# Moving a pair's residual behind the zeroing in VectorE's queue, with the softmax sums in a layout for fewer DMAs

## The chip, the cores and the metric

The kernel runs on one core of one Trainium2 chip. The metric is the device time of one execution in microseconds (us); lower is better. Before the change it is 2849.32 us, the median of three runs (2841.83 to 2855.34).

## The reference

Two layers of attention over images of 16 x 256 x 32 x 32 in float32. In each layer the input is normalised in 16 groups over the last axis, projected to queries, keys and values of 4 heads (64 channels each), and attended with a relative position term; the result is added to the input.

```python
q, k, v = proj(Wq, bq), proj(Wk, bk), proj(Wv, bv)      # b, heads, 64, 1024
sim = jnp.einsum('bhdi,bhdj->bhij', q, k)
rel = (rel_h + rel_w).reshape(heads, d, n)
qpos = jnp.einsum('hdi,bhdj->bhij', rel, q)
attn = jax.nn.softmax(sim + qpos, axis=-1)
out = jnp.einsum('bhdn,bhmn->bhdm', v, attn)
...
x = x + _L0_conv_ref(_gn(x), ...)
x = x + _L1_conv_ref(_gn(x), ...)
```

## The kernel before, in words

The work is cut into 32 units, one per image and layer. A unit has two pairs of heads (`pr`), and a pair has two halves of 512 query positions, so a unit is four blocks; in `block(n)` the variable `b` is 0 to 3 and `half` is `b` modulo 2. The text calls them the first to the fourth block. The order of instructions on each engine is written out by hand: each engine works through its own queue strictly in the order in which `block` emits, and semaphores connect the queues. Moving a call in `block` therefore moves that instruction in its engine's queue and nothing else.

A block makes eight tiles of scores (`j` = 0 to 7), each of 128 keys by 2 heads by 512 queries. VectorE first writes the position term into PSUM (`seed`, L343), TensorE adds the products of keys and queries (`scores`, L379), and ScalarE takes exp into SBUF with a fixed shift in place of a maximum (L388). VectorE adds the eight tiles up in an accumulator (`add_up`, L397 and L399). TensorE multiplies the eight tiles with the values into `po`, in two stretches (`attend`, L413). The four two-bank PSUM tiles are called by the names in `ring`; a seed has to wait until ScalarE has read what stood in its tile before.

Between these stand pieces of later work: the projections, values and positions of the next pair or unit (`prepare`, L262, L292, L320), and the normalisation of the unit after the next, which is done by ScalarE (L187, L242). Its mean and its variance each take a small product on TensorE (`pm`, L207). That product adds into PSUM, so VectorE zeroes `pm` first (`zeroed`, L199). This happens in the third block for the mean and in the fourth for the variance. ScalarE then takes `neg` (L217) or `var` (L229) out of `pm`; the tile is one that the next block's second seed uses. GpSimd computes `rstd` and `nshift` from the variance (L231, L233). `token` (L163) is a tiny memset on GpSimd that keeps the two stretches of a product apart.

The softmax sums of a pair come out as follows. GpSimd's accumulating DMA folds the accumulator from 128 to 64 partitions (`fold`, L432); SyncE's DMA puts one quarter of it in the pair's `stack` (`stack_up`, L441); GpSimd's accumulating DMA adds the other quarter (`fold_again`, L448). One block after the pair's end, TensorE sums the stack over its partitions into the unused halves of `po` (`sums_of_pair`, L460). ScalarE copies `po` to `od` (`take_out`, L474 and L478): slots 0 and 1 of `od` hold the output of the two halves, slot 2 the sums. SyncE's DMAs spread the sums over 128 partitions in `den_all` (L485), VectorE takes reciprocals of 16 numbers per partition (`reciprocals`, L519), and SyncE's DMAs write them to `rd` in device memory (L522) and read them back, repeated over 64 partitions each, into `rden` (L525). All DMAs that SyncE issues leave in their order in its queue, and one whose source isn't ready holds up those behind it. Finally VectorE multiplies the output with `rden` and adds it with the bias to the image (`finish`, L536 and L537), the residual of the text. This is done once per pair, in the block with `half` = 1 of the following pair, so in each second and fourth block, for the pair `before`.

The last unit's second pair has no later work to interleave and is done by `block_without_pieces`.

Of the kernel before, what the change touches and what calls it, by code (L numbers as in the profile page):

```python
# [9 lines left out]
F32 = mybir.dt.float32  # L10
# [7 lines left out]
P = 128  # L18
HALF = 512
# [33 lines left out]
def fast_path(ctx, tc, sh, x, layers, out, W, den_all, token, good, flag):  # L53
# [26 lines left out]
    nc = tc.nc  # L80
    B, C, H, N, CC, NT, NH, D, GT = (
        sh.B, sh.C, sh.H, sh.N, sh.CC, sh.NT, sh.NH, sh.D, sh.GT
    )
# [317 lines left out]
    QUART = HALF // 2  # L401
# [32 lines left out]
    def stack_up(blk):  # L434

        u, pr, x = blk
        if x == 0:
            stacks[u, pr] = spool.tile([P, HALF], F32, tag="stack", name=f"stack_{u}_{pr}")
        for h in range(2):
            r0 = x * D + h * R  # L440
            nc.sync.dma_start(stacks[u, pr][r0 : r0 + R, :], accs[blk][:R, h, :])  # L441

    def fold_again(blk):
        u, pr, x = blk
        acc = accs.pop(blk)
        for h in range(2):
            r0 = x * D + h * R
            nc.gpsimd.dma_start(  # L448
                stacks[u, pr][r0 : r0 + R, :], acc[R:D, h, :], accum_op=ALU.add
            )  # L450

    def sums_of_pair(u, pr, po):

        stack = stacks.pop((u, pr))
        for x, rs in enumerate(QUARTERS):
            for c, cs in enumerate(QUARTERS):
                nc.tensor.matmul(  # L460
                    po[cs, 1 - x, QUART:],
                    W.two_ones[rs, :],
                    stack[rs, c * QUART : (c + 1) * QUART],
                    start=True, stop=True, skip_group_check=True,
                )

    def take_out(blk, po, sums_too=False):

        u, pr, half = blk
        if half == 0:  # L470
            outs[u, pr] = opool.tile([P, 3, HALF], F32, tag="od", name=f"od_{u}_{pr}")
        od = outs[u, pr]
        if not sums_too:
            nc.scalar.copy(  # L474
                od[:, half, :].rearrange("p (a n) -> p a n", a=2), po[:, :, :QUART]
            )
            return
        nc.scalar.copy(  # L478
            od[:, 0:3:2, :].rearrange("p z (a n) -> p z a n", a=2),
            po.rearrange("p a (z n) -> p z a n", z=2),  # L480
        )
        n = index[blk] - 2
        for x in range(2):
            for h in range(2):
                nc.sync.dma_start(  # L485
                    den_all[h * D : (h + 1) * D, n + x, :],
                    od[h * R : P : D, 2, (1 - x) * QUART : (2 - x) * QUART],
                )

    def sums_of_p(two, po):  # L490

# [22 lines left out]

    def reciprocals(u, pr, count=2):

        n = index[u, pr, 0]
        r8 = fpool.tile([P, 2, 8], F32, tag="r8", name=f"r8_{u}_{pr}")
        nc.vector.reciprocal(r8[:, :count, :], den_all[:, n : n + count, :])  # L519
        rd = dpool.tile([2, 2, HALF], F32, tag="rd", name=f"rd_{u}_{pr}")  # L520
        for x in range(count):
            nc.sync.dma_start(rd[:, x, :].rearrange("h (a b) -> h a b", b=8), r8[:, x, :])  # L522
        rdens[u, pr] = opool.tile([P, 2, HALF], F32, tag="rden", name=f"rden_{u}_{pr}")
        for h in range(2):
            nc.sync.dma_start(  # L525
                rdens[u, pr][h * D : (h + 1) * D, :count, :],
                rd[h : h + 1, :count, :].to_broadcast([D, count, HALF]),
            )

    def finish(u, pr):  # L530

        b, l = units[u]
        xs = xt[b][:, pr, :]
        o = outs.pop((u, pr))[:, 0:2, :].rearrange("p a n -> p (a n)")
        rden = rdens.pop((u, pr)).rearrange("p a n -> p (a n)")
        nc.vector.tensor_tensor(o, o, rden, ALU.mult)  # L536
        nc.vector.scalar_tensor_tensor(xs, o, W.bv[l][:, pr : pr + 1], xs, ALU.add, ALU.add)  # L537
        if l == NL - 1:
            nc.sync.dma_start(flat(out[b, pr * P : (pr + 1) * P]), xs)
# [75 lines left out]
    def block(n):  # L615
        blk = blocks[n]
        u, b = divmod(n, BPU)
        half = blk[2]
        before = blocks[n - 3][:2] if half == 1 and n > 2 else None
        after = blocks[n + 1] if n + 1 < len(blocks) else None  # L620
        previous = blocks[n - 1] if n > 0 else None
        one, two = u + 1 < NU, u + 2 < NU

        pieces = u + 1 < NU or b < 2
        if u + 1 == NU and b == 1:
            widen(u, 1)
        f0, f1, f2, f3 = ring
        folded = n - 1 < FOLDED
        if not pieces:
            return block_without_pieces(n, half)  # L630

        if previous:
            if half == 0:
                add_up(previous, 6)
            add_up(previous, 7)
        for j in range(1, 4):
            scores(blk, j)
        if b == 3 and u + 3 < NU and units[u + 3][0] not in xt:
            load_x(units[u + 3][0])
        (first, first_out), (second, second_out) = prepare(u, b)  # L640
        first(0)
        if b == 0 and one:
            norm_apply(u + 1, range(0, 1))
        if b == 2 and two:
            norm_sums(u + 2, range(8, 11))
        if b == 3 and two:
            norm_squares(u + 2, range(6, 9))
        seed(blk, 4, f1)
        scores(blk, 4)
        add_up(blk, 1)  # L650
        if before:
            reciprocals(*before)
        if half == 0:
            add_up(blk, 2)
        if b == 0 and one:
            norm_apply(u + 1, range(1, 5))
        if b == 1 and one:
            norm_apply(u + 1, range(15, G))
        if b == 2 and two:
            norm_sums(u + 2, range(11, G))  # L660
        if b == 3 and two:
            norm_squares(u + 2, range(9, 13))
        second(0)
        if half == 1:
            second_out()
        first.word()
        if previous and folded:
            fold(previous)
            stack_up(previous)
        first(1)  # L670
        first_out()
        seed(blk, 5, f0)
        scores(blk, 5)
        if half == 0:
            add_up(blk, 3)
            second.word()
            if previous and folded:
                fold_again(previous)
            second(1)
            second_out()  # L680
        seed(blk, 6, f1)
        scores(blk, 6)
        if half == 0:
            ring[2:] = f3, f2
        seed(blk, 7, ring[2])
        scores(blk, 7)
        if half == 1:
            add_up(blk, 2)
            add_up(blk, 3)
        add_up(blk, 4)  # L690

        if after:
            seed(after, 0, f0)
        if before:
            finish(*before)
        if n in check:
            next(checks)
        if b == 0 and one:
            norm_apply(u + 1, range(5, 10))
        if b == 3 and two:  # L700
            norm_squares(u + 2, range(13, G))
        po = psum2(ring[3], f"po_{n}")
        values_of_p = attend(blk, po)
        values_of_p(0)
        if two and b >= 2:
            mean, mean_out = (norm_mean if b == 2 else norm_var)(u + 2, zeroed(f1, f"pm_{n}"))
            mean(0)
        if after:
            scores(after, 0)
        values_of_p.word()  # L710
        if two and b >= 2:
            mean(1)
            values_of_p.word()
            mean_out()
        add_up(blk, 5)
        if after:
            for j in range(1, 4):
                seed(after, j, ring[j % 3])
        if half == 0:
            add_up(blk, 6)  # L720
        if b == 0 and one:
            norm_apply(u + 1, range(10, 15))
        if b == 1 and two:
            norm_sums(u + 2, range(0, 8))
        if b == 2 and two:
            norm_squares(u + 2, range(0, 6))
        values_of_p(1)
        if half == 1:
            if folded:
                fold_again(previous)  # L730
            take_out(blk, po)
            pos[n] = po
            return
        if n > 1:
            sums_of_pair(*blocks[n - 2][:2], po)
        take_out(blk, po, n > 1)
# [8 lines left out]
    def block_without_pieces(n, half):  # L745
# [43 lines left out]
        pd = psum2(f0, "pd")  # L789
        sums_on_rows(acc, pd)  # L790
        values_of_p(1)
        finish_half(u, pr, 0, outs[u, pr][:, 0, :], rdens[u, pr][:, 0, :])
        rden = rdens[u, pr][:, 1, :]
        nc.vector.reciprocal(rden, pd[:, 0, :])
        pd = psum2(f2, "pd_columns")[:, 0, : 2 * HALF // P]
        sums_on_columns(acc, pd)
# [417 lines left out]
```

## Time and profile before

| | |
|---|---|
| Time, median of 3 runs | 2849.32 us |
| Profiled execution, from first to last instruction | 2845.8 us |
| Mean granted TensorE clock | 0.981 |
| VectorE, 128 x 1024 float32 (L343, L399) | 1.23 and 1.22 us each |
| ScalarE, exp of 128 x 1024 (L388) | 1.12 us each |
| ScalarE, copy of 128 x 512 and 128 x 1024 (L474, L478) | 0.58 and 1.01 us each |
| VectorE, residual: L536, L537 | 1.22 and 1.29 us each, 63 of both |
| VectorE, memset of `pm` (L199) | 0.07 us each, 60 of them |
| SyncE, issue of one DMA (L485, L522, L525) | 0.57, 0.52 and 0.51 us, medians |

The profile is of one execution. In it, PE is TensorE's matmuls, PEld its weight loads, DVE VectorE, ACT ScalarE, POOL GpSimd and SPq the queue in which SyncE issues DMAs. A line of the list of waits names who waited for whom: engine, tile and line, then the total in us, the number of waits and the longest. A line of a timeline has the start, the time taken, the engine, the line and operation, the tiles (written on the left of the arrow, read on the right) and how many of the same stand together; in brackets stands how long the engine was idle before it and what released it. A line of busy time by stretch has the stretch, its length, each engine's busy time and number of instructions, the granted clock of TensorE (1.00 is full speed), the share of DMA and GB/s. A memset of zero takes so little time that a wait for it means a wait for what stands before it in its queue.

### The profile page before, as it was taken

Reading aid. Unit: us, or ns where it says so; the run is one execution under the profiler, and the core shown is the slowest. Engines: PE = TensorE matmul, PEld = TensorE weight load, DVE = VectorE, ACT = ScalarE, POOL = GpSimd, SP = SyncE. Lnnn points to the kernel's source line nnn. Section 1 sums busy time; section 2 is a strip of 40 time slices with the busy share of each in tenths; the row PEclk is TensorE's granted clock in tenths of the full one; section 3 lists DMA queues with packets and bytes.
Section 4 is the critical chain, followed back from the end, with each engine's and each line's share of the span. In section 5 each row is a group of like instructions: output and inputs, shape, how many; then the busy total and the mean of one; then the engine's idle time right before and its main releaser. Section 6 shows DMA issues by size and latency. Waiting matters only on the chain.

```text
span 2845.8 us, 86631 instructions
## 1 busy us (share of the span) xinstructions
PE 2642.4 (93%) x37970; PEld 1468.8 (52%) x37970; DVE 2427.1 (85%) x2200; ACT 1980.7 (70%) x3934; POOL 476.0 (17%) x825
## 2 busy tenths in 40 slices
PE   8999999899898999999999999999999989999998
PEld 4545555455454554545545555465554545545545
DVE  7888888888888888888888888888888888889898
ACT  6767677676676766767767667677676767767754
POOL 1111211111111111111111111111111111121110
PEclk9999999999999999999999999999999999999999
DMA  2122121221212212122131222222222222222221
GB/s 77 32 56 43 34 69 34 63 49 33 69 35 62 48 33 69 36 63 47 34 71 35 62 45 45 63 40 56 45 52 57 40 54 47 41 53 39 43 57 44
DMA packets 91615, 140.27 MB, mean 49 GB/s; under 512 B 49374, under 2 KB 50910, under 8 KB 91230
## 3 DMA queue, kind: packets, MB, share of 16 engines
q0 software_dynamic: 21824, 48.78, 11.7%
q1 hardware_dynamic: 69406, 85.88, 11.1%
q8 instruction: 299, 4.90, 0.7%
q14 instruction: 86, 0.70, 0.1%
HBM read 51.78 MB, written 17.30 MB: 24 GB/s over the span
## 4 chain that ended last, share of the span: by engine, by line
PE 45%; DVE 26%; DMA 16%; issue 6%; SPq 4%; ACT 4%; DVEq 0%; POOL 0%; POOLq 0%
PE po L413 16%; PE ps L379 14%; DVE ps L343 13%; DMA rden<-rd 7%; DVE acc L399 7%; DMA rd<-r 7%; PE pq L262 6%; PE pk L262 4%; PE pv L292 3%; DVE x L537 3%; DVE od L536 3%; DMA den_all<-od 2%; SPq L485 2%; ACT od L478 1%; SPq L525 1%
## 5 line engine op out<-in xcount | busy, mean ns | idle before, releaser
L388 ACT ACTIVATE p<-ps,shift 128x1024 f32<-128x1024 f32 x1024 | 1098.6, 1115 | 597.9 <-PE ps L379 322.7
L343 DVE TENSOR_TENSOR ps<-abt 128x1024 f32<-128x1024 f32 x1018 | 1223.4, 1227 | 335.3 <-ACT neg L217 118.6
L379 PE MATMUL ps<-q,k 64*64 64x512 f32 x8192 | 1041.4, 604 | 78.1 <-DVE ps L343 71.0
L413 PE MATMUL po<-p,v 64*64 64x256 f32 x16384 | 962.2, 384 | 0.0
L399 DVE TENSOR_TENSOR acc<-acc,p 128x1024 f32<-128x1024 f32 x768 | 938.1, 1222 | 19.1 <-ACT p L388 0.5
L413 PEld LDWEIGHTS po<-p,v 64*64 64x64 f32 x16384 | 704.5, 136 | 289.1 <-issue 60.0
L379 PEld LDWEIGHTS ps<-q,k 64*64 64x64 f32 x8192 | 314.7, 134 | 523.6 <-DVE ps L343 268.9
L163 POOL MEMSET token<- 1x1 f32 x380 | 34.0, 89 | 1944.1 <-PE po L413 722.1
L292 PE MATMUL pv<-Wv,xn 64*64 64x256 f32 x4096 | 246.8, 376 | 0.3 <-DVE var L862 0.3
L262 PE MATMUL pq<-xn,Wq 64*64 64x512 f32 x2048 | 245.3, 593 | 0.3 <-DVE xn L894 0.3
L262 PE MATMUL pk<-xn,Wk 64*64 64x512 f32 x2048 | 244.0, 590 | 0.0
L448 POOL DMA_DIRECT2D stack<-acc x248 | 198.2, 926 | 258.3 <-DMA stack<-acc 246.3
L292 PEld LDWEIGHTS pv<-Wv,xn 64*64 64x64 f32 x4096 | 174.5, 133 | 80.8 <-issue 47.5
L242 ACT ACTIVATE xn<-x,nshift,rstd 128x128 f32<-128x128 f32 x496 | 210.3, 496 | 0.0
L187 ACT ACTIVATE junk<-x,neg 128x128 f32<-128x128 f32 x498 | 196.2, 403 | 1.0
L397 DVE TENSOR_TENSOR acc<-p,p 128x1024 f32<-128x1024 f32 x128 | 155.9, 1218 | 0.0
L262 PEld LDWEIGHTS pq<-xn,Wq 64*64 64x64 f32 x2048 | 81.8, 134 | 138.9 <-issue 133.7
L187 ACT ACTIVATE junk<-x 128x128 f32<-128x128 f32 x480 | 143.4, 304 | 1.3 <-DVE x L537 1.3
L262 PEld LDWEIGHTS pk<-xn,Wk 64*64 64x64 f32 x2048 | 78.4, 134 | 122.1 <-issue 121.8
L231 POOL TENSOR_TENSOR rstd<-var,mhalf 128x16 f32<-128x16 f32 x30 | 118.9, 3963 | 78.7 <-ACT var L229 78.7
L207 PE MATMUL pm<-sum,avg 64*64 64x16 f32 x240 | 20.1, 233 | 105.5 <-DVE pm L199 105.5
L432 POOL DMA_DIRECT2D acc<-acc x124 | 100.0, 806 | 60.6 <-DVE ps L343 20.9
(78 smaller groups left out, 1109.3 us busy)
## 6 DMA issues: line engine op xcount, KB each, us to landing
rden<-rd SPq DMA_DIRECT2D x126, 256.0 KB
acc<-acc POOLq DMA_DIRECT2D x124, 256.0 KB, 3.5
x<-in_x_dram SPq DMA_DIRECT2D x32, 512.0 KB
stack<-acc SPq DMA_DIRECT2D x248, 64.0 KB
stack<-acc POOLq DMA_DIRECT2D x248, 64.0 KB, 2.6
out_dram<-x SPq DMA_DIRECT2D x31, 512.0 KB
den_all<-od SPq DMA_DIRECT2D x254, 2.0 KB
rd<-r SPq DMA_DIRECT2D x127, 4.0 KB
```

The costliest lines, as they stand in the source:

```text
L187: nc.scalar.activation(junk, grouped(xt[units[u][0]], g), func, accum_out=into[:, g : g + 1], **bias)
L231: nc.gpsimd.tensor_tensor(rstd, var, W.mhalf[:, :G], ALU.pow)
L242: nc.scalar.activation(grouped(xns[u], g), grouped(xt[units[u][0]], g), AF.Identity, bias=shift[:, g : g + 1], scale=rstd[:, g : g + 1],)
L262: yield nc.tensor.matmul(pk[c, nh, :], w[l][rs, cc, c0 : c0 + D], xns[u][rs, cc, nh * HALF : (nh + 1) * HALF], start=(t == 0 and cc == 0), ...
L292: yield nc.tensor.matmul(pv[c, a, i, :], xns[u][rs, cc, j0 : j0 + D], W.wv[l][rs, cc, :], start=(t == 0 and cc == 0 and i == 0), stop=(t = ...
L343: nc.vector.tensor_tensor(ps.rearrange("p h (w y) -> p h w y", y=H), ab[:, :, :H].unsqueeze(2).to_broadcast([P, 2, XH, H]), ab[:, :, H + h ...
L379: nc.tensor.matmul(ps[c, h, :], a[hs, j0 : j0 + D], b[hs, columns], start=bool(tag) and i == 0, stop=i == len(terms) - 1, skip_group_check ...
L388: nc.scalar.activation(p, ps, AF.Exp, bias=W.shift)
L397: nc.vector.tensor_tensor(accs[blk], probs[blk, 0], probs[blk, 1], ALU.add)
L399: nc.vector.tensor_tensor(accs[blk], accs[blk], probs[blk, j], ALU.add)
L413: yield nc.tensor.matmul(po[c, a, :QUART], vts[u][rs, j, c0 : c0 + D], p[rs, h, a * QUART : (a + 1) * QUART], start=(t == 0 and j == 0), s ...
L448: nc.gpsimd.dma_start(stacks[u, pr][r0 : r0 + R, :], acc[R:D, h, :], accum_op=ALU.add)
```

## The change

1. In `block`, `finish(*before)` moves from right after the next block's first seed to after `add_up(blk, 5)`, which stands behind the zeroing of `pm` and in front of the next block's three other seeds.
2. In blocks with `half` = 0, `add_up(previous, 7)` moves behind the fourth seed of the block, and `add_up(blk, 6)` moves in front of the next block's three seeds.
3. In blocks with `half` = 1, `fold_again(previous)` moves from the block's end to in front of `mean_out`.
4. The sums of a pair are laid out with the two blocks interleaved in runs of 8 numbers, so that one row of `od` holds both blocks' sums for one head. ScalarE takes the sums out first, by a copy of their own that does the interleaving, and the output with a second copy. Two DMAs in place of four then fill `den_all`, and one in place of two writes `rd`; `rden` is read back in the interleaved order, and the multiply of the residual reads it in runs of 8. The two halves of `stack` change places.

The aim of 1 and 2 is that what TensorE waits for comes earlier in VectorE's queue; of 3 and 4, that the sums and reciprocals arrive earlier.

```diff
     def stack_up(blk):
...
-            r0 = x * D + h * R
+            r0 = (1 - x) * D + h * R
             nc.sync.dma_start(stacks[u, pr][r0 : r0 + R, :], accs[blk][:R, h, :])
...
     def take_out(blk, po, sums_too=False):
...
-        nc.scalar.copy(
-            od[:, 0:3:2, :].rearrange("p z (a n) -> p z a n", a=2),
-            po.rearrange("p a (z n) -> p z a n", z=2),
-        )
-        n = index[blk] - 2
-        for x in range(2):
-            for h in range(2):
+        if sums_too:
+            nc.scalar.copy(
+                od[:, 2, :].rearrange("p (k x e) -> p k x e", x=2, e=8),
+                po[:, :, QUART:].rearrange("p x (k e) -> p k x e", e=8),
+            )
+            n = index[blk] - 2
+            for h, hs in enumerate(QUARTERS):
                 nc.sync.dma_start(
-                    den_all[h * D : (h + 1) * D, n + x, :],
-                    od[h * R : P : D, 2, (1 - x) * QUART : (2 - x) * QUART],
+                    den_all[hs, n : n + 2, :].rearrange("p x e -> p (x e)"),
+                    od[h * R : P : D, 2, :],
                 )
+        nc.scalar.copy(od[:, half, :].rearrange("p (a n) -> p a n", a=2), po[:, :, :QUART])
...
     def reciprocals(u, pr, count=2):
...
-        rd = dpool.tile([2, 2, HALF], F32, tag="rd", name=f"rd_{u}_{pr}")
-        for x in range(count):
-            nc.sync.dma_start(rd[:, x, :].rearrange("h (a b) -> h a b", b=8), r8[:, x, :])
+        rd = dpool.tile([P, count * 8], F32, tag=f"rd{count}", name=f"rd_{u}_{pr}")
+        nc.sync.dma_start(rd, r8[:, :count, :].rearrange("p x e -> p (x e)"))
...
     def finish(u, pr):
...
-        rden = rdens.pop((u, pr)).rearrange("p a n -> p (a n)")
+        rden = rdens.pop((u, pr)).rearrange("p (k x e) -> p x k e", x=2, e=8)
         nc.vector.tensor_tensor(o, o, rden, ALU.mult)
...
     def block(n):
...
         if previous:
-            if half == 0:
-                add_up(previous, 6)
-            add_up(previous, 7)
+            add_up(previous, 6 if half == 0 else 7)
...
         seed(blk, 4, f1)
+        if previous and half == 0:
+            add_up(previous, 7)
         scores(blk, 4)
...
         if after:
             seed(after, 0, f0)
-        if before:
-            finish(*before)
...
         if two and b >= 2:
             mean(1)
-            values_of_p.word()
+        if previous and folded and half == 1:
+            fold_again(previous)
+        if two and b >= 2:
             mean_out()
         add_up(blk, 5)
+        if before:
+            finish(*before)
+        if half == 0:
+            add_up(blk, 6)
         if after:
             for j in range(1, 4):
                 seed(after, j, ring[j % 3])
-        if half == 0:
-            add_up(blk, 6)
...
         if half == 1:
-            if folded:
-                fold_again(previous)
             take_out(blk, po)
```

More of the change, by code (lines that the diff above doesn't have):

```diff
@@ L446, in fold_again @@
         for h in range(2):
-            r0 = x * D + h * R
+            r0 = (1 - x) * D + h * R
             nc.gpsimd.dma_start(
@@ L457, in sums_of_pair @@
         stack = stacks.pop((u, pr))
-        for x, rs in enumerate(QUARTERS):
+        for rs, x in BANKS[1]:
             for c, cs in enumerate(QUARTERS):
                 nc.tensor.matmul(
-                    po[cs, 1 - x, QUART:],
+                    po[cs, x, QUART:],
                     W.two_ones[rs, :],
@@ L472, in take_out @@
         od = outs[u, pr]
-        if not sums_too:
+        if sums_too:
             nc.scalar.copy(
-                od[:, half, :].rearrange("p (a n) -> p a n", a=2), po[:, :, :QUART]
-            )
-            return
-        nc.scalar.copy(
-            od[:, 0:3:2, :].rearrange("p z (a n) -> p z a n", a=2),
-            po.rearrange("p a (z n) -> p z a n", z=2),
-        )
-        n = index[blk] - 2
-        for x in range(2):
-            for h in range(2):
+                od[:, 2, :].rearrange("p (k x e) -> p k x e", x=2, e=8),
+                po[:, :, QUART:].rearrange("p x (k e) -> p k x e", e=8),
+            )
+            n = index[blk] - 2
+            for h, hs in enumerate(QUARTERS):
                 nc.sync.dma_start(
-                    den_all[h * D : (h + 1) * D, n + x, :],
-                    od[h * R : P : D, 2, (1 - x) * QUART : (2 - x) * QUART],
+                    den_all[hs, n : n + 2, :].rearrange("p x e -> p (x e)"),
+                    od[h * R : P : D, 2, :],
                 )
+        nc.scalar.copy(od[:, half, :].rearrange("p (a n) -> p a n", a=2), po[:, :, :QUART])
     def sums_of_p(two, po):
@@ L519, in reciprocals @@
         nc.vector.reciprocal(r8[:, :count, :], den_all[:, n : n + count, :])
-        rd = dpool.tile([2, 2, HALF], F32, tag="rd", name=f"rd_{u}_{pr}")
-        for x in range(count):
-            nc.sync.dma_start(rd[:, x, :].rearrange("h (a b) -> h a b", b=8), r8[:, x, :])
-        rdens[u, pr] = opool.tile([P, 2, HALF], F32, tag="rden", name=f"rden_{u}_{pr}")
-        for h in range(2):
+        rd = dpool.tile([P, count * 8], F32, tag=f"rd{count}", name=f"rd_{u}_{pr}")
+        nc.sync.dma_start(rd, r8[:, :count, :].rearrange("p x e -> p (x e)"))
+        rden = opool.tile([P, 2 * HALF], F32, tag="rden", name=f"rden_{u}_{pr}")
+        rdens[u, pr] = rden
+        rd = rd.rearrange("(h k) e -> h (k e)", h=2)
+        for h, hs in enumerate(QUARTERS):
             nc.sync.dma_start(
-                rdens[u, pr][h * D : (h + 1) * D, :count, :],
-                rd[h : h + 1, :count, :].to_broadcast([D, count, HALF]),
+                rden[hs, : count * HALF],
+                rd[h : h + 1].to_broadcast([D, count * HALF]),
             )
@@ L533, in finish @@
         xs = xt[b][:, pr, :]
-        o = outs.pop((u, pr))[:, 0:2, :].rearrange("p a n -> p (a n)")
-        rden = rdens.pop((u, pr)).rearrange("p a n -> p (a n)")
+        od = outs.pop((u, pr))
+        o = od[:, 0:2, :].rearrange("p x (k e) -> p x k e", e=8)
+        rden = rdens.pop((u, pr)).rearrange("p (k x e) -> p x k e", x=2, e=8)
         nc.vector.tensor_tensor(o, o, rden, ALU.mult)
+        o = od[:, 0:2, :].rearrange("p a n -> p (a n)")
         nc.vector.scalar_tensor_tensor(xs, o, W.bv[l][:, pr : pr + 1], xs, ALU.add, ALU.add)
@@ L791, in block_without_pieces @@
         values_of_p(1)
-        finish_half(u, pr, 0, outs[u, pr][:, 0, :], rdens[u, pr][:, 0, :])
-        rden = rdens[u, pr][:, 1, :]
+        finish_half(u, pr, 0, outs[u, pr][:, 0, :], rdens[u, pr][:, :HALF])
+        rden = rdens[u, pr][:, HALF:]
         nc.vector.reciprocal(rden, pd[:, 0, :])
```

## The prediction

> **What bounds the kernel now.** I read the busy shares first, then the list of waits, then the timelines of TensorE and VectorE around the longest wait, then busy time and granted clock by stretch.
>
> ```profile
> PE 2642.4 (93%) x37970; PEld 1468.8 (52%) x37970; DVE 2427.1 (85%) x2200; ACT 1980.7 (70%) x3934; POOL 476.0 (17%) x825
> ```
>
> TensorE is busy for all but 203 us, so what can be gained is its idle time and its slow time. The list of waits says who causes the idle time:
>
> ```profile
> DVE ps L343 <- ACT neg L217: 118.6, 30, 4.0
> ...
> PE pm L207 <- DVE pm L199: 105.5, 30, 5.3
> ...
> PE ps L379 <- DVE ps L343: 71.0, 106, 1.8
> ...
> DVE ps L343 <- ACT var L229: 64.7, 30, 2.6
> ...
> DVE od L536 <- DMA rden<-rd: 33.8, 44, 2.4
> ```
>
> Thirty times (once a unit, in its fourth block) TensorE waits 3.5 us on average for a memset of 72 ns. One such unit, TensorE and then VectorE:
>
> ```profile
> 1078.00 3.63 PE L413 MATMUL po<-p,v 64*64 64x256 f32 x64
> 1086.35 0.29 PE L207 MATMUL pm<-sum,avg 64*64 64x16 f32 x2 [4.71 <-DVE pm L199]
> ```
>
> ```profile
> 1080.60 1.23 DVE L343 TENSOR_TENSOR ps<-abt 128x1024 f32<-128x1024 f32 x1
> 1083.58 1.23 DVE L536 TENSOR_TENSOR od<-od,rden 128x1024 f32<-128x1024 f32 x1 [1.75 <-DMA rden<-rd]
> 1084.84 1.28 DVE L537 SCALAR_TENSOR_TENSOR x<-od,bv,x 128x1024 f32<-128x1024 f32 x1
> 1086.06 1.25 DVE L399 TENSOR_TENSOR acc<-acc,p 128x1024 f32<-128x1024 f32 x1
> 1086.13 0.07 DVE L199 MEMSET pm<- 128x16 f32 x1
> 1089.90 1.23 DVE L343 TENSOR_TENSOR ps<-abt 128x1024 f32<-128x1024 f32 x1 [2.58 <-ACT var L229]
> ```
>
> The memset stands behind the residual (L536, L537), which itself stood 1.75 us for a DMA. Without a DMA wait the TensorE stall is 2.86 us, the commonest value. Afterwards VectorE idles 2.58 us, because the next seed needs the memset's buffer, which ScalarE frees with `var`: the queue has its work in the wrong order.
>
> ```profile
> 1081.60:1086.30 4.70, 0.03 (x4) 0.00 (x0) 2.91 (x5) 0.00 (x0) 0.09 (x1) 0.73 0.23 48
> 1086.30:1088.50 2.20, 2.15 (x20) 1.33 (x24) 1.01 (x1) 0.00 (x0) 0.09 (x1) 0.50 0.59 238
> 1088.50:1093.00 4.50, 4.50 (x69) 3.22 (x68) 3.10 (x3) 1.28 (x2) 3.05 (x1) 0.77 0.01 4
> 1093.00:1097.00 4.00, 4.00 (x58) 2.01 (x52) 3.96 (x5) 3.58 (x4) 3.16 (x4) 1.00 0.23 24
> ```
>
> The column before the last two is the clock: at the end of the stall it halves, for 6.8 us. The means and the 64 matmuls of `po` that follow take 2.1 + 4.6 us here; in the third block, at full clock, 1.0 + 3.45.
>
> [...] stalls of 2.86 to 5.35 us, clock 0.50, none elsewhere in the steady part; gaps under 2 us show 1.00. [...] the trace shows only that the old took 3.65 us quiet and 5.65 us behind a load of x. [...] the prologue's multiply over runs of two floats (L894) takes 1758 ns for 1536 elements, 1.14 ns each, against 1223/1024 = 1.19 at L536.
>
> **The change, part by part, for one unit of four blocks.** The reference is the unit that starts its third block's scores at 2627.90 and the next at 2714.36: 86.46 us, clock 1.00 throughout, stall 2.86. Over the 29 units from 158.44 to 2714.36 the mean is 88.14.
>
> *Residual behind the memset (fourth block).* VectorE ends the next block's first seed about 0.2 us after TensorE ends the first stretch of `po` (1081.83 against 1081.64). Memset 0.07, and 0.22 from its start to TensorE's (1086.13, 1086.35): a stall of about 0.6 remains, 2.26 less. Residual (1.24 + 1.28) and add 5 (1.14) now fill the gap in which VectorE waits for `var`: TensorE's means and scores take 1.0, exp 1.0, `var` 0.27, with handovers 2.6 us after the memset; add and residual take 3.7. So the three seeds come 1.1 us later after the memset than `var` would allow. TensorE meanwhile does the second stretch of `po`, 3.45 us, and then the three scores at 0.86 each while the seeds come every 1.14: about 0.75 lost. The reference loses 0.69 at the following seed 4 instead, which goes, since an add now stands behind that seed. Net +0.06.
>
> *Residual in the second block.* Add 5 moves in front of the residual, where VectorE waited for the DMA (0.36 us at 1038.76). The seeds start 0.4 earlier; TensorE's wait at the third block's first scores falls from 0.65 to 0.25. Gain 0.4.
>
> *One add moved behind seed 4, add 6 in front of the seeds.* In even blocks two adds (2.4 us) stood before seed 4, now one: TensorE's 0.72 wait there goes, with 0.2 of spacing before it, 0.9. Add 6 of the third block now runs in the wait for `neg` (4.0 us), so the fourth block's seed 4 comes 1.14 earlier and its 0.36 wait (71.06 against 70.7) goes. In the first block add 6 fills a wait for exp (1.8 us at 1022.06): nothing.
>
> *Fewer DMAs.* Two stores to `den_all` (0.57 each) and one to `rd` (0.53) fewer to issue: 1.7 us. The first copy out of `po` is 0.58 instead of 1.01 before the sums can leave. In the fourth block the reciprocal ran at 1072.05 and `rden` landed at 1083.48, 11.4 later, or 10.9 with one issue less. The chain's transfer of 5.65 can become anything down to the 1.64 of `den_all`; I take no gain from it. With everything about 2.4 earlier, `rden` lands at 1080.5 on that clock and the residual starts at 1081.3: no wait, with 0.8 to spare. A second copy on ScalarE, 2 x 0.58 for 1.01, is hidden, since ScalarE has 30% idle; it delays exp by 0.1.
>
> *Accumulating DMAs earlier on GpSimd.* Two issues of 0.8 now stand before `rstd`; `var` comes 3.0 us after the token, which hides them. If they wait for the stack's DMA (2.7 us on average elsewhere), `rstd` is late by about 1.3; its reader has 3.0 us (nshift ends at 1004.5, xn starts at 1007.57). Nothing.
>
> *Sum.* 86.46 - 2.26 + 0.06 - 0.4 - 0.9 - 0.36 = 82.6; the feed-in of fourth-block seed 7 (0.57, `abt` on ScalarE) stays. About 0.2 of handover goes with the moved adds, since adds on one accumulator take 1.25 back to back and 1.14 apart: 82.4. No stall then exceeds 0.8 us, so the clock stays at 1.00. Saving over the mean unit 88.14 - 82.4 = 5.75, thirty times: 172 us. 2849 - 172 = 2677; the last units' other waits give about 2 more: **2675 us**. Check by rows: 105.5 to 18 saves 87; the clock's deficit is 0.019 x 2846 = 55 us, of which 1.27 of 3.41 lay in the idle time of the long case: 34 to 55 saved, say 42; 1.3 a unit at the third block's start 40; 0.36 a unit 11; against 6 more in the first block: 174.
>
> VectorE's work per unit stays 75.3 us, 91% of 82.4, and its order leaves it only 7 us of waits, so small misjudgements show.
>
> **Rivals.** *The wait moves to the seeds* (chance 0.20). Three seeds are queued behind the residual and TensorE's next scores wait for them. If `rden` comes as late as its worst wait (2.4), or the ties above fall badly, 2 us a unit return: 84.4, 2849 - 30 x 3.75 = 2737. For it: VectorE at 91%. Against: 0.8 of slack and 10.9 taken without the faster store. *The low clock has another cause* (0.07): stalls go, 42 us stay, 2717. Against: each low stretch follows a stall. *The strided layout is dear* (0.05): VectorE's reciprocal (L794) shows 3351/512 = 6.5 ns an element; a multiply at that rate costs 6.7 us, 5.5 more, twice a unit, 11 - 5.75 with 2 hidden: +3.3 x 30, **2947, slower**. Against: L894. *DMA-bound anyway, nothing moves* (0.02): 2845.
>
> **How the numbers follow.** The forecast takes the remaining 0.66. Without any TensorE wait a unit would be about 80.1 us, 2606, which is out of reach with `abt` and the ties left; half of those 2.3 us won gives 2640. The upper end takes in the low clock and part of the moved wait: 2728. Faster by over 0.5%: 0.66 + 0.20 + 0.07 = 0.93; same 0.02; slower 0.05.
>
> **What would show it.** Right: TensorE's wait for L199 near 18 us, clock about 1.00, the wait for `rden` near 0, the waits for `neg` and `var` shorter, L343 as a releaser of TensorE 50 to 70 us and now at the first block's scores. Wrong: L538 (the multiply) over 1.3 us, a wait for `rden` in the fourth block, seeds releasing TensorE for over 100 us, or clock still 0.98.

## The result, and the profile after

The changed kernel takes 2669.68 us, the median of four runs (2669.09 to 2670.76). The kernel before took 2847.76 us beside it. The ratio is 0.9374, 95% interval 0.9351 to 0.9397: 178 us or 6.3% less. The forecast was 2675.

The busy shares of the changed kernel:

```profile
span 2667.9 us, 86560 instructions
...
PE 2608.5 (98%) x37970; PEld 1412.8 (53%) x37970; DVE 2407.3 (90%) x2200; ACT 1992.4 (75%) x3996; POOL 466.5 (17%) x825
```

The 178 us between the profiled spans (2845.8 and 2667.9) can be found in TensorE's row and its waits. The list of waits of the changed kernel:

```profile
PEld ps L379 <- DVE ps L343: 334.6, 561, 1.5
...
DVE ps L343 <- ACT neg L217: 65.8, 30, 2.5
...
PE ps L379 <- DVE ps L343: 22.9, 63, 0.6
...
PE pm L207 <- DVE pm L199: 10.8, 30, 0.4
```

TensorE's wait for the zeroing fell from 105.5 to 10.8, so 94.7 us. Its wait for seeds fell from 71.0 to 22.9, so 48.1 us. Its busy time for the same 37970 matmuls fell from 2642.4 to 2608.5, so 33.9 us. Together that is 176.7 of the 177.9 us. VectorE's waits for `rden` (33.8 before) and for `var` (64.7) are gone from the list.

The fall in busy time is a net figure. The mean granted clock rose from 0.981 to 0.999, and this alone is worth more. From the means to the end of the second stretch of `po`, the thirty fourth blocks took 177.7 us before; at full clock, as in seven of them, one takes 4.45 us, so all would take 133.5. The slow clock cost 44.2 us there. In the changed kernel the same stretches take 139.3 us, and the three scores behind them take 95.4 in place of 77.4. These 24 us are waits for seeds, but they lie inside TensorE's busy time: matmul after matmul is recorded as busy, and the wait is recorded at the weight load in front. The next three scores of one unit show it, first before and then in the changed kernel, with one of the weight loads (the third line):

```profile
1092.89 2.77 PE L379 MATMUL ps<-q,k 64*64 64x512 f32 x24
1099.12 3.36 PE L379 MATMUL ps<-q,k 64*64 64x512 f32 x24
1100.25 0.21 PEld L379 LDWEIGHTS ps<-q,k 64*64 64x64 f32 x8 [0.92 <-DVE ps L343]
```

The 44.2 less these 24 leave 20 of the 33.9; the other 13 or so are spread over other stretches and were not followed up.

VectorE and then TensorE at the end of one fourth block, by the timeline:

```profile
1093.08 1.23 DVE L343 TENSOR_TENSOR ps<-abt 128x1024 f32<-128x1024 f32 x1
1094.23 1.21 DVE L399 TENSOR_TENSOR acc<-acc,p 128x1024 f32<-128x1024 f32 x1
1094.26 0.07 DVE L199 MEMSET pm<- 128x16 f32 x1
1095.36 1.22 DVE L538 TENSOR_TENSOR od<-od,rden 128x1024 f32<-128x1024 f32 x1
1096.61 1.28 DVE L540 SCALAR_TENSOR_TENSOR x<-od,bv,x 128x1024 f32<-128x1024 f32 x1
1097.81 3.52 DVE L343 TENSOR_TENSOR ps<-abt 128x1024 f32<-128x1024 f32 x3
```

```profile
1090.48 3.63 PE L413 MATMUL po<-p,v 64*64 64x256 f32 x64
1094.47 0.23 PE L207 MATMUL pm<-sum,avg 64*64 64x16 f32 x2 [0.36 <-DVE pm L199]
```

The memset now follows the seed at once, TensorE waits 0.36 us where it had waited 4.71, and the residual (L538 and L540 here) fills the time in which VectorE used to wait for `var`. The stretch behind the wait, by busy time, shows full clock in the column before the last two:

```profile
1094.40:1100.00 5.60, 5.53 (x88) 3.79 (x88) 5.57 (x5) 1.86 (x3) 4.58 (x4) 1.00 0.17 23
```

SyncE's issues by the timeline, the store to `rd` and the read-back, first in the kernel before and then in the changed kernel, both with no load of x near:

```profile
673.29 1.09 SPq L522 DMA_DIRECT2D rd<-r  x2
677.54 1.15 SPq L525 DMA_DIRECT2D rden<-rd  x2
```

```profile
632.19 0.32 SPq L521 DMA_DIRECT2D rd<-r  x1
633.64 1.75 SPq L526 DMA_DIRECT2D rden<-rd  x2
```

From the first issue of the store to the issue of the read-back that waits for it, 4.25 us became 1.45. Behind a load of x it went from 6.30 (1072.32 to 1078.62) to 3.51 (672.78 to 676.29).

### The profile page after: what moved, and what is told of

The parts are those of the page before. It is cut to its first block, busy times and chain, and to the rows that moved or that the text cites. A ratio compares the mean times of both kernels' runs of the same rounds, so it can differ in the third digit from the quotient of the medians.

```text
span 2667.9 us, 86560 instructions
## 1 busy us (share of the span) xinstructions
PE 2608.5 (98%) x37970; PEld 1412.8 (53%) x37970; DVE 2407.3 (90%) x2200; ACT 1992.4 (75%) x3996; POOL 466.5 (17%) x825
## 4 chain that ended last, share of the span: by engine, by line
PE 56%; DVE 29%; ACT 8%; issue 5%; DMA 3%; SPq 0%; POOL 0%; DVEq 0%; POOLq 0%
PE ps L379 18%; PE po L413 17%; DVE ps L343 11%; DVE acc L399 10%; PE pq L262 8%; PE pk L262 6%; PE pv L292 4%; DVE x L540 3%; DVE od L538 3%; ACT p L388 3%; ACT junk L187 2%; ACT abt L331 2%; DMA den_all<-od 2%; DVE acc L397 1%; PE po L460 1%
## 5 line engine op out<-in xcount | busy, mean ns | idle before, releaser
L379 PE MATMUL ps<-q,k 64*64 64x512 f32 x8192 | 1038.7, 598 | 28.6 <-DVE ps L343 22.9
L413 PE MATMUL po<-p,v 64*64 64x256 f32 x16384 | 933.5, 377 | 0.0
L413 PEld LDWEIGHTS po<-p,v 64*64 64x64 f32 x16384 | 674.0, 133 | 289.6 <-issue 61.4
L379 PEld LDWEIGHTS ps<-q,k 64*64 64x64 f32 x8192 | 296.4, 132 | 500.6 <-DVE ps L343 334.6
L163 POOL MEMSET token<- 1x1 f32 x380 | 33.8, 89 | 1795.0 <-PE po L413 696.0
L292 PEld LDWEIGHTS pv<-Wv,xn 64*64 64x64 f32 x4096 | 176.5, 133 | 80.4 <-issue 49.7
L397 DVE TENSOR_TENSOR acc<-p,p 128x1024 f32<-128x1024 f32 x128 | 155.6, 1216 | 0.0
L485 ACT COPY od<-po 128x512 f32<-128x512 f32 x127 | 74.7, 589 | 75.5 <-PE po L413 75.5
L231 POOL TENSOR_TENSOR rstd<-var,mhalf 128x16 f32<-128x16 f32 x30 | 108.2, 3607 | 3.2
```

The source lines that it names most:

```text
L231: nc.gpsimd.tensor_tensor(rstd, var, W.mhalf[:, :G], ALU.pow)
L292: yield nc.tensor.matmul(pv[c, a, i, :], xns[u][rs, cc, j0 : j0 + D], W.wv[l][rs, cc, :], start=(t == 0 and cc == 0 and i == 0), stop=(t = ...
L379: nc.tensor.matmul(ps[c, h, :], a[hs, j0 : j0 + D], b[hs, columns], start=bool(tag) and i == 0, stop=i == len(terms) - 1, skip_group_check ...
L397: nc.vector.tensor_tensor(accs[blk], probs[blk, 0], probs[blk, 1], ALU.add)
L413: yield nc.tensor.matmul(po[c, a, :QUART], vts[u][rs, j, c0 : c0 + D], p[rs, h, a * QUART : (a + 1) * QUART], start=(t == 0 and j == 0), s ...
```

## Experiments

Theory: what TensorE waits for, the zeroing and the seeds, stood behind work in VectorE's queue for which nobody waits; the order is what pays, and the halved clock is a consequence of the long stall. Rivals: the fewer DMAs pay, by bringing `rden` early; or the half clock is what pays, or doesn't pay at all.

| Kernel | us | Ratio to the kernel before |
|---|---|---|
| changed kernel | 2669.7, again 2670.4 | 0.9374, again 0.9386 |
| e1: residual back in its old place | 2764.4 | 0.9725 |
| e2: residual alone moved | 2735.3 | 0.9623 |
| e3, e10: all moves, old DMAs | 2674.7, again 2677.3 | 0.9413, again 0.9408 |
| e4: adds alone moved | 2809.0 | 0.9877 |
| e7: new DMAs alone | 2804.8 | 0.9866 |

The intervals are within 0.0023 of each ratio. The kernel before was 2841.4 to 2847.8 us beside them.

### The residual put back

```diff
             seed(after, 0, f0)
+        if before:
+            finish(*before)
...
         add_up(blk, 5)
-        if before:
-            finish(*before)
```

> The changed kernel with one part undone: the residual stands again in front of the zeroing. Theory (the order of VectorE's queue sets TensorE's stall): the wait for the zeroing returns to 2.9 us a unit in all thirty units, never more, since rden is now early; 75 us of stall and 0 to 50 us of half clock come back: 2745 to 2795 us, clock 0.98 to 0.99. Rival (the fewer DMAs are what pays): under 2700 us, stall near 0.4 us.

Measured: 2764.4 us, 94.7 more than the changed kernel. Its list of waits:

```profile
PE pm L207 <- DVE pm L199: 86.5, 30, 3.3
```

The stall is back at 2.9 us a unit, 75.7 us more, though `rden` is early. TensorE's busy time is 2634.8 us, 26.3 more, at a clock of 0.979. These two sum to 102, against 99.1 between the profiled spans. (The 26.3 are net as well: the stretches from the means to the end of `po` take 183.2 us, so the slow clock costs 49.7 here, and the 24 us of waits inside the busy time are gone.) The rival under which the fewer DMAs are what pays falls.

### The residual alone moved

```diff
-        if before:
-            finish(*before)
         if n in check:
...
         add_up(blk, 5)
+        if before:
+            finish(*before)
```

> The kernel before with the residual alone moved behind the zeroing and add 5; adds and DMAs as before. Theory: stall 0.4 to 0.6 us, clock 1.00, the third block's waits of 0.7 + 0.4 us stay: 2700 to 2725 us. Rival (without the fewer DMAs the residual waits for rden in its new place and holds up the seeds): over 2740 us, with VectorE waiting for rden and TensorE for seeds in the first block.

Measured: 2735.3 us, 106.6 less than the kernel before and 10 above the range that was expected. Its waits:

```profile
PE ps L379 <- DVE ps L343: 73.6, 130, 1.4
...
PE pm L207 <- DVE pm L199: 10.9, 30, 0.4
...
DVE od L536 <- DMA rden<-rd: 5.5, 7, 1.3
```

The stall is gone and the clock is 0.999. The rival's sign, a wait for `rden`, is small. What the expectation had missed stands in the first row: TensorE's timeline shows a wait of 0.71 to 0.74 us for seed 4 in the first block, besides 0.72 in the third. In the changed kernel add 7 stands behind these seeds and both waits are gone.

### All moves with the old DMAs

The functions `stack_up` to `finish` are those of the kernel before, `block` is that of the changed kernel.

> The changed kernel with the old layout of sums and reciprocals, so the old DMAs: four to den_all and two to rd a pair, one copy of 128 x 1024. All moves of instructions stay. Theory (the DMAs are hidden once the residual stands later): 2665 to 2685 us, VectorE's wait for rden under 10 us in all. Rival (the early arrival is needed): over 2700 us with waits for rden in the fourth block.

> The kernel e3_dmas_back unaltered, beside the changed kernel on one chip. Theory (DMAs nearly hidden, with rden late in a few units): 3 to 8 us above the changed kernel. Rival (fully hidden): within 2 us of it.

> The changed kernel unaltered, on one chip with the next three, so that a difference of 5 us can be read: 2665 to 2674 us.

Measured: 2674.7 us, and on one chip 2677.3 beside 2670.4 for the changed kernel, 6.8 us more. The list of waits of e10:

```profile
DVE r L519 <- DMA den_all<-od: 12.6, 58, 0.8
...
DVE od L536 <- DMA rden<-rd: 5.7, 6, 2.3
```

`rden` is late six times, by up to 2.3 us, and the reciprocal waits some 0.2 us for most pairs. So the fewer DMAs are nearly but not fully hidden.

### Adds alone, and DMAs alone

```diff
         if previous:
-            if half == 0:
-                add_up(previous, 6)
-            add_up(previous, 7)
+            add_up(previous, 6 if half == 0 else 7)
...
         seed(blk, 4, f1)
+        if previous and half == 0:
+            add_up(previous, 7)
...
         add_up(blk, 5)
+        if half == 0:
+            add_up(blk, 6)
```

> The kernel before with the two adds alone moved (add 7 behind seed 4, add 6 in front of the seeds). Theory (the third block's wait at seed 4 is worth 0.9 us a unit and the fourth block's 0.36): 2805 to 2822 us. Rival (what is won there is lost at the zeroing, which is set by rden): 2840 us or more.

For the DMAs alone, the functions `stack_up` to `finish` are those of the changed kernel and `block` is that of the kernel before.

> The kernel before with the new layout of sums and reciprocals alone, so the fewer DMAs; order of VectorE unchanged. Theory: rden comes before the residual wants it, the stall falls to its floor of 2.86 us in every unit (0.66 less on average), 0.3 us less in the second block, fewer long low clocks: 2810 to 2832 us. Rival (DMAs hidden anyway): 2845 us or more.

Measured: 2809.0 us for the adds, 32 less than the kernel before, as expected. TensorE's wait for seeds is 39.1 instead of 71.0, and the stall is unchanged (104.7). The DMAs alone give 2804.8 us, 36.5 less and a little more than expected. The waits of e7:

```profile
PE pm L207 <- DVE pm L199: 87.2, 30, 3.4
...
PE ps L379 <- DVE ps L343: 50.6, 104, 0.7
...
DVE od L538 <- DMA rden<-rd: 0.8, 2, 0.5
```

With the residual in its old place, a late `rden` stands straight in front of the zeroing, so an early one is worth 18.3 us there and 20.4 at the seeds. With the residual moved, the same DMAs are worth 6.8. The adds go the other way: 32 alone, but 60.6 between e2 and e3 (where GpSimd's accumulating DMAs move as well; no run moves those by themselves). Two things make the difference. TensorE's idle time falls by 37.0 us in e4 and by 52.0 from e2 to e3, its wait for seeds alone by 31.9 and by 47.8: the wait for seed 4 in the first blocks is 25.8 us in e2 and 5.7 in the kernel before, where a slow TensorE mostly comes too late to meet it. And its busy time falls by 0.3 us in e4 and by 11.3 from e2 to e3: the clock of e4 is 0.974, and its stretches from the means to the end of `po` take 191.7 us, 14.0 more than in the kernel before.

### The halved clock: filling the stall

TensorE gets matmuls of no use between the first stretch of `po` and the means, into a half of `po` that nobody reads in that block. In e5 `range` is 10, in e5b it is 5.

```diff
         values_of_p(0)
+        if two and b == 3:
+            for k in range(10):
+                for rs, a in BANKS[0]:
+                    for h, c in enumerate(QUARTERS):
+                        nc.tensor.matmul(
+                            po[c, a, QUART:],
+                            vts[u][rs, 0, blk[1] * P + h * D : blk[1] * P + (h + 1) * D],
+                            probs[blk, 0][rs, h, :QUART],
+                            start=False, stop=True, skip_group_check=True,
+                        )
```

> The kernel before, order unchanged, with 40 more matmuls of 64 x 256 (about 2.2 us) in each of the thirty stalls, into a half of po that nobody reads. They shorten no wait for the zeroing but leave TensorE idle for only the rest. Theory (the half clock comes of the idle stretch): clock 1.00 nearly everywhere and 25 to 42 us less: 2807 to 2825 us. Rival (another cause): clock 0.98, 2845 us or more.

> The kernel before with half as many filler matmuls (about 2.15 us, below the shortest stall of 2.86; in e5_warm_filler they took 4.31 us and lengthened what they filled). Theory (half clock comes of idle time and costs some 20 to 35 us here, since a warm TensorE meets a wait of 0.7 us for seed 4 in the first block that a slow one doesn't): clock 1.00, 20 to 35 us under the kernel before. Rival (the clock costs nothing, since something else sets the end): within 5 us.

Both missed. e5 takes 2838.3 us, ratio 0.999 (0.9983 to 0.9997), at a clock of 0.999. The filler was twice as long as meant, 4.31 us, so it made a stall of 3.5 us longer on average. e5b takes 2835.3 us, 9.0 less than the kernel before, ratio 0.9964 (0.9951 to 0.9977). The clock of e5b and then its waits:

```profile
core 0: 2836.6 us, clock 0.994
```

```profile
PE ps L379 <- DVE ps L343: 79.6, 116, 1.3
...
PE pm L207 <- DVE pm L199: 50.5, 30, 4.0
DVE od L536 <- DMA rden<-rd: 42.7, 46, 3.2
```

That the clock follows the idle stretch is shown by e5: with the stall filled the clock is 0.999 in place of 0.981, and VectorE's order is unchanged. In e5b, where stalls of up to 4.0 us remain, it is 0.994. There the stretches from the means to the end of `po` fall from 177.7 to 147.5 us, so some 30 us of slow time are gone, but most of what this gives is lost again. Filler (30 x 2.15) and remaining wait make 115 us against 105.5, the seeds cost 8.6 more, and VectorE waits 8.9 more for `rden`: TensorE reaches the next wait earlier and waits longer there. So of the 30 us of slow time that e5b removes, 9 are left as a gain; the rest is to be had only with the waits gone too.

### The halved clock: lengthening the stall

The reverse, on the changed kernel: two (e8) or six (e8b) adds on VectorE, of no use, in front of the zeroing.

```diff
         values_of_p(0)
+        if two and b == 3:
+            for i in range(2):
+                idle = apool.tile([P, HALF], F32, tag="idle", name=f"idle_{n}_{i}", bufs=1)
+                nc.vector.tensor_tensor(idle, probs[blk, 0][:, 0, :], probs[blk, 1][:, 0, :], ALU.add)
```

> The changed kernel with two adds of 128 x 512 of no use put in front of the zeroing of each fourth block, so about 1.2 us of TensorE stall more in thirty units. Theory [...]: clock 1.00, 2669.7 + 36 = 2700 to 2712 us. Rival (VectorE sets the end and any work on it counts twice, or waits absorb it): clearly more or less than 36.

> As e8_stall_1p2 but six adds of no use, so three times as much stall, about 4 us in each fourth block. e8_stall_1p2 cost 41.8 us for 41.3 us of stall. Theory [...]: 124 us of stall and 25 to 55 us of slow matmuls, 2818 to 2850 us, clock 0.96 to 0.98. Rival (a stall costs itself whatever its length): 2790 to 2798 us.

Measured: e8 takes 2711.5 us, 41.8 more than the changed kernel, at a clock of 0.999. Its wait for the zeroing is 52.1 us, 41.3 more (1.7 a unit). e8b takes 2846.7 us, 176.3 more. Its wait and its clock:

```profile
PE pm L207 <- DVE pm L199: 139.3, 30, 4.6
```

```profile
core 0: 2846.2 us, clock 0.966
```

128.5 us of that are stall; TensorE's busy time is 2661.4, 52.9 more than in the changed kernel. (The stretches from the means to the end of `po` take 210.0 us, so the slow clock costs 76.5; 24 of that take the place of the waits inside the busy time.) Thirty stalls of up to 1.7 us cost what they added and no more (41.8 us for 41.3); thirty of up to 4.6 us cost 1.4 times what they added (176.3 for 128.5). e8b is as slow as the kernel before (ratio 1.0004, 0.9996 to 1.0013): a single late memset a unit can undo all that the change gained.

### A version that goes further

Three more moves in the fourth block: ScalarE takes `abt` out before four of the squares, the zeroing stands in front of the next block's first seed, and add 5 stands behind the three other seeds.

```diff
-        if b == 3 and two:
-            norm_squares(u + 2, range(9, 13))
         second(0)
         if half == 1:
             second_out()
+        if b == 3 and two:
+            norm_squares(u + 2, range(9, 13))
...
+        turned = b == 3 and two
+        pm = zeroed(f1, f"pm_{n}") if turned else None
         if after:
             seed(after, 0, f0)
...
-        add_up(blk, 5)
+        if not turned:
+            add_up(blk, 5)
...
                 seed(after, j, ring[j % 3])
+                if turned and j == 3:
+                    add_up(blk, 5)
```

> The changed kernel with three more moves in each fourth block: ScalarE takes abt out before four of the squares; the zeroing stands in front of the next block's first seed; add 5 stands behind the three seeds. Theory: the waits of 0.56 us (abt), 0.36 us (zeroing) and some 0.75 us (seeds behind add and residual) go: 30 x 1.0 to 1.6, so 2620 to 2645 us. Rival (VectorE at 90% has become the bound): no gain, 2660 to 2690 us.

Measured: 2653.6 us, ratio 0.9335 (0.9320 to 0.9351), 16 less than the changed kernel. That lies between the range that was expected (2620 to 2645) and the rival's (2660 to 2690). TensorE's timeline at the next first block shows why:

```profile
1015.29 1.09 PE L379 MATMUL ps<-q,k 64*64 64x512 f32 x8 [0.74 <-DVE ps L343]
...
1020.03 1.09 PE L379 MATMUL ps<-q,k 64*64 64x512 f32 x8 [0.20 <-DVE ps L343]
```

The waits of 0.56 for `abt` and of 0.36 for the zeroing are gone. But add 5 went where adds hurt: two adds stand again in front of seed 4, and its wait of 0.7 us is back, with 0.2 at seed 5. VectorE's amount of work, 91% busy here, was not yet the bound, since a change of order alone still gained.

## Why the prediction was right, and where it was off

The working went by one unit: 86.46 us without slow clock, 88.14 in the mean, 82.4 forecast. Measured between the third blocks that start at 1057.32 and 2538.67, it is 82.30 for each of 18 units. The remaining 5 us of difference are mostly this 0.1 a unit, thirty times.

- *Residual behind the memset.* About 0.6 us of stall was to remain; 0.36 did, as the memset begins with the seed's end. The loss at the next block's first three scores was put at 0.75: the matmuls that follow the second stretch take 3.17 us from 1099.12 to 1102.29 instead of 2.58, after 0.2 of waiting, 0.79. That the reference's wait for seed 4 there goes was right; e2 shows it in reverse.
- *Residual in the second block.* 0.65 to 0.25 was forecast; 0.18 remains.
- *Adds.* The wait of 0.72 at the third block's seed 4 and the 0.36 in the fourth block are gone, as said. VectorE's wait for `neg` is 65.8 instead of 118.6, filled by add 6.
- *DMAs.* The step said that `rden` would be in time without a faster transfer. It is nearly right: e10, which has no faster transfer, is late in six units and 6.8 us slower in all. Taking no gain from the transfer left out what it really gained, 2.8 us for each store to `rd` (4.25 to 1.45). The prediction's 3.65 and 5.65 us are the store to `rd` of the kernel before, from its second issue (1030.23 and 1072.89). What makes the single store faster was not shown.
- *Clock.* 42 us were put on it in the check by rows, and 44.2 is what the slow clock had cost behind the stalls. TensorE's busy row fell by 33.9 only, as waits moved into it. The stall's term, 87, was too low by 8 (94.7). With thirty stalls of up to 1.7 us (e8) the mean clock is 0.999, with thirty of up to 4.6 (e8b) 0.966. Between these the length alone doesn't tell: stalls of 2.86 to 2.87 us halved the clock in 8 of 13 units of the kernel before, and e1, whose thirty stalls are 2.9 us on average, is at 0.979. The prediction read "stalls of 2.86 to 5.35 us, clock 0.50" and passed over the seven units, with stalls of 2.86 to 3.15 us, that stayed at 1.00; its own reference unit is one. The last section says what decided.
- *What the profile would show.* Seeds were to release TensorE for 50 to 70 us in its own row; it is 22.9. With the 24 us that lie inside the busy time, seeds hold TensorE up for some 47 us, and for more with the third block's first scores (3.18 us from 1057.32 in place of 2.58). The row of weight loads that wait for seeds grew from 268.9 to 334.6 us, but most of that passes while matmuls run, as TensorE is idle for only 59.4 us in all. The sign looked at one row alone, which shows half of the wait or less.
- *Layout.* The multiply reads runs of 8 floats in 1216 ns against 1223 before, so the slower rival had no ground. GpSimd's two earlier issues delay nothing: `rstd` starts at 1097.08, when `var` is out (1096.73 + 0.27).

The rival in which the wait moves to the seeds was true in kind for 0.8 us a unit, which the forecast contained, not for the 2 us on which it would have ended at 2737.

## What to carry to other kernels

When an engine waits for an instruction of almost no length, look at what stands ahead of it in its queue, and put in front of it only work for which somebody waits as soon; work that nobody needs for long belongs into the next place where that queue idles anyway. Gains of such moves don't add: the DMAs were worth 36.5 us alone and 6.8 at the end, the adds 32 alone and some 60 at the end, so judge each with the others in place. A row of busy time can contain waits (24 us here) and slow time (44.2 us before), so measure the stretch itself, from one start to the next. Work the new unit out instruction by instruction from the old timeline, with what every engine waits for, and start from a unit that no slow clock disturbs.

## What had not been expected of the hardware

A store of 128 x 16 numbers to device memory in one DMA is done 1.45 us after its issue, where two of 2 x 64 x 8 took 4.25 us from the first issue, read by the issue of the read-back that waits for them. The medians of all 64 pairs are 1.46 and 4.27. Behind a load of x the single store took 3.51, so what else is under way counts. The issue takes 0.32 us instead of 0.52. Taking away 30 us of slow matmul time by itself, with idle time filled, gave 9.0 us.

And the same stall did not always halve the clock: in the kernel before, stalls of 2.86 to 2.87 us did so in 8 units and not in 5. What set these apart was where the stall fell. In the clock records of this trace the 23 low stretches before the one at the program's end last 3.41 or 6.83 us, and all 24 start whole multiples of 3.413 us apart, so a grid of that step can be laid through them. The first two lines are the stretch of the grid that holds 2.33 us of the stall of 2.87 that ends at 111.51, and the one after it, at half clock. The third holds 1.66 us of the stall of 2.86 that ends at 2668.76, with the other 1.20 in the stretch after it; the clock stays at 1.00.

```profile
107.56:110.97 3.41, 1.08 (x21) 0.46 (x12) 3.38 (x4) 0.31 (x2) 0.09 (x1) 1.00 0.01 2
110.98:114.38 3.40, 2.87 (x28) 1.79 (x32) 1.50 (x3) 0.63 (x1) 0.09 (x1) 0.50 0.02 5
2664.14:2667.55 3.41, 1.76 (x36) 0.92 (x25) 3.38 (x4) 0.99 (x6) 0.09 (x1) 1.00 0.16 32
```

The kernel before has thirty such waits for the zeroing. The clock halved at each of the 23 that put 2.08 us or more into one stretch of the grid, and at none of the 7 that put 2.02 us or less there. So in this trace the border lies between 2.02 and 2.08 us of idle time in one stretch, and whether a stall of 2.86 us trips it depends on its place. Why it does was not shown.
